# Score products of a Perceiver kernel: all products of a PSUM bank ahead of its reductions, low part last

## The chip, the cores and the metric

The kernel runs on one core of a Trainium2 chip. The metric is the time of one execution on the device in microseconds (us). Before the change three runs gave 2074.91, 2084.85 and 2086.65 us, a median of 2084.85.

## The reference

The input `x` has 8 batches of 64 tokens with 512 features; the context has 8 batches of 1601 rows with 512 features. Three layers follow one another, each with a residual. The change lies in the first, in its cross attention:

```python
kvx = jnp.einsum('bsi,oi->bso', cond, w_kv_x)        # cond is the context
kx, vx = jnp.split(kvx, 2, axis=-1)
kx = _ln(kx.reshape(b, sc, g, d), kxln_w, kxln_b)    # g = 8 groups, d = 128
vx = vx.reshape(b, sc, g, d)
xout = _gqa(qx, kx, vx).reshape(b, s, nh * d)        # nh = 16 heads, two per group
...
def _gqa(q, k, v):
    scores = jnp.einsum('bsghd,btgd->bghst', q, k) / np.sqrt(q.shape[-1])
    p = jax.nn.softmax(scores, axis=-1)
    return jnp.einsum('bghst,btgd->bsghd', p, v)
```

The same layer also has a self attention and a projection with values rounded to fp8; the second layer is a sparse attention with a learned pair score; the third is a feed-forward network with ternary weights.

## The kernel before

**Work items.** The cross attention is cut into 16 objects of class `Cross`, one for each batch and each half of the eight groups (`HG` = 4 groups in a half). In each group the 128 query rows are two heads of 64 tokens. The 1601 context rows are 13 tiles of 128 rows (`TT`, the last of 65), gathered into six chunks (`CHUNKS`): five of two tiles, so 256 columns, and a last one of three, 321 columns, padded to 322.

**One tile's way.** `keys` (L515 on) loads a transposed context tile, splits it into a high part `cThi` (ACT) and the rest `cTlo` (POOL), and multiplies it by the key weights, which are split in the same way: 12 matmuls of 512 columns into a bank `kx` (L528). ACT squares, DVE sums (L534), POOL takes the inverse root (`rqk`, L173), and DVE writes the normalized keys `kn` (L537). One step later `keys_t` transposes `kn` with four PE transposes into another bank `kx` (L219), ACT writes the keys' high part `kthi` (L550), DVE the difference `kf` (L552), ACT the low part `ktlo` (L553). When all tiles of a chunk are there, `scores` makes, for each of the four groups, three products: high queries by high keys (L571), high queries by low keys (L572), low queries by high keys (L573). A reduction on DVE (L574) then copies the group's scores from PSUM to the tile `S` and takes each row's maximum into `cmx`.

**What follows.** 17 steps behind (`LAG`), ACT exponentiates `S` (L584), `probs_t` transposes a tile of it into a bank `pt` (L593), which is split into `phi` (ACT, L596) and `plo` (DVE, L597), and `weigh` multiplies these by the context tile's parts `chi` and `clo` into four banks `acc` (L620 to L622).

**Banks.** PSUM has eight banks of 512 float32 columns a partition. Pool `pm` holds three (`mainp`): scores `s`, transposed probabilities `pt`, and, once `lane["wide"]` is off, the key tiles `kx` (`kxp`) take turns in them. Pool `pacc` holds four, the sums `acc` over the context; pool `pb` holds one for the background work. In a chunk of 256 columns two groups share a bank (`per` = 2), which makes 160 shared banks over the whole run; in the last chunk each group has its own, 64 in all.

**Order.** The main loop walks over all tiles of all work items and calls the steps in a software pipeline; the other layers' work is pumped in between from streams. The order on each engine is chosen when the kernel is built, by a scheduler with its own costs (`schedule_with_timeline_sim=True`), which may place ready instructions ahead of others. It also inserts the waits: an instruction that writes a tile waits for those that still read or write it.

Of the kernel before, what the change touches and what calls it, by code (L numbers as in the profile page):

```python
# [17 lines left out]
ALU = mybir.AluOpType  # L18
# [3 lines left out]
P = 128  # L22
# [7 lines left out]
HG = 4  # L30
# [7 lines left out]
NCH = len(CHUNKS)  # L38
# [19 lines left out]
def tile_perceiver(ctx: ExitStack, tc: tile.TileContext, t: dict):  # L58
    nc = tc.nc
    V, A, GP, PE = nc.vector, nc.scalar, nc.gpsimd, nc.tensor  # L60
# [16 lines left out]
    def nm(s):  # L77
        uid[0] += 1
        return f"{s}_{uid[0]}"

    def ctile(shape, dt, tag):
        return const.tile(shape, dt, tag=tag, name=tag)
# [9 lines left out]
    def mainp(tag="m"):  # L92
        return pm.tile([P, 512], F32, tag="m", name=nm(tag))

    def kxp(tag="kx"):


        if lane["late"] is not None:
            return lane["late"]
        return accp(tag) if lane["wide"] else mainp(tag)  # L100
# [41 lines left out]
    class Late:  # L142
# [13 lines left out]
        ps = staticmethod(lambda tag="b": kxp())  # L156
# [68 lines left out]
    zeros = ctile([P, 1], F32, "zeros")  # L225
# [268 lines left out]
    class Cross:  # L494
# [60 lines left out]
        def scores(self, ci):  # L555
            chunk = CHUNKS[ci]
            cw = sum(TT[tt][1] for tt in chunk)
            hi, lo = self.kt.pop(ci)
            N = cw + (cw & 1)
            if N > cw:  # L560
                GP.memset(hi[:, :, cw:N].bitcast(F32), 0.0)
                GP.memset(lo[:, :, cw:N].bitcast(F32), 0.0)
            sc = mp.tile([P, HG, KTW], F32, tag="S", name=nm("S"), bufs=7)
            self.S[ci] = sc
            per = 512 // N
            for g in range(HG):
                if g % per == 0:
                    bank = mainp("s")
                ps = bank[:, g % per * N:(g % per + 1) * N]
                q = slice(g * P, (g + 1) * P)  # L570
                PE.matmul(ps, lhsT=self.qhi[:, q], rhs=hi[:, g, :N], start=True, stop=False)  # L571
                PE.matmul(ps, lhsT=self.qhi[:, q], rhs=lo[:, g, :N], start=False, stop=False)  # L572
                PE.matmul(ps, lhsT=self.qlo[:, q], rhs=hi[:, g, :N], start=False, stop=True)  # L573
                V.tensor_tensor_reduce(sc[:, g, :cw], ps[:, :cw], zeros.to_broadcast([P, cw]), 1.0, -3.0e38,  # L574
                                       ALU.add, ALU.max, self.mx[:, g * NCH + ci:g * NCH + ci + 1])

        def maxima(self):
            self.nmx = sm("cnm", HG)
# [472 lines left out]
    for g in range(NA + LAG + 3):  # L1051
# [11 lines left out]
        if 0 <= e < NA:  # L1063
# [4 lines left out]
            ci = CHUNK_OF[kE]  # L1068
# [15 lines left out]
        if 0 <= g - 2 < NA:  # L1084
            nS, kS = divmod(g - 2, NT)
            ci = CHUNK_OF[kS]
# [130 lines left out]
```

## Time and profile before

| | |
|---|---|
| median of three runs | 2084.85 us (2074.91 to 2086.65) |
| profiled execution | 2083.31 us, its span 2081.6 us |
| granted TensorE clock | 0.988 of full speed |
| PE busy | 1979.7 us, 95% |
| PE weight loads (PEld) | 1633.8 us, 78% |
| DVE, ACT, POOL busy | 67%, 63%, 46% |
| DMA | 257.34 MB, mean 124 GB/s |
| score products, L571, L572, L573 | 112.7, 109.4 and 109.0 us busy, 384 each |
| score reductions, L574, two shared-bank groups and the last chunk's | 157.1 us busy, 384, 429 ns each |

PE is TensorE's matmul row, PEld its weight loads, which overlap matmuls; DVE is VectorE, ACT ScalarE, POOL GpSimd. A matmul is pipelined: its row's duration reaches beyond the start of the next one, so a busy PE is not a PE at its peak. A wait is idle time of an engine before an instruction, put down to what released it last.

### The profile page before, as it was taken

The numbers are of one execution on the slowest core, as the hardware profiler recorded it, in microseconds if no ns is written. First come the engines' busy times: TensorE is split into PE (matmuls) and PEld (weight loads), VectorE is DVE, ScalarE is ACT, GpSimd is POOL, SyncE is SP. The second block draws the span as 40 slices with busy tenths as digits, with TensorE's granted clock in tenths as the row PEclk, the third lists the DMA queues.
The fourth block names the chain that finished last, engine by engine and source line by source line (L and its number), as shares of the span: only waits on it lengthen the run. The fifth ranks groups of instructions, "written<-read, shape, count | busy, mean of one in ns | idle before, by whom it ended". The sixth has DMA issues, their size and how long they took to land. (4 is left out here: it accounts for less than half of the span.)

```text
span 2081.6 us, 32709 instructions
## 1 busy us (share of the span) xinstructions
PE 1979.7 (95%) x10923; PEld 1633.8 (78%) x10923; DVE 1390.4 (67%) x3344; ACT 1304.4 (63%) x2787; POOL 952.9 (46%) x1018
## 2 busy tenths in 40 slices
PE   5889999999999899999999999999999999999998
PEld 4778878888778788887888888787878778877776
DVE  7876676576676775767777777675755665576665
ACT  5666757677666666665656656666556665566554
POOL 5454545454454444445444544444454445542232
PEclk9999999999999999999999999999999999999999
DMA  5443343444334444544544454432433223333325
GB/s 180 127 116 112 113 124 110 122 135 127 107 117 130 140 144 123 173 133 156 161 142 148 142 176 145 142 106 69 127 104 109 77 77 97 87 93 101 114 69 170
DMA packets 261817, 257.34 MB, mean 124 GB/s; under 512 B 25408, under 2 KB 186304, under 8 KB 261648
## 3 DMA queue, kind: packets, MB, share of 16 engines
q1 hardware_dynamic: 261648, 255.25, 41.1%
q8 instruction: 86, 1.41, 0.3%
q14 instruction: 83, 0.68, 0.1%
HBM read 231.33 MB, written 23.59 MB: 122 GB/s over the span
## 5 line engine op out<-in xcount | busy, mean ns | idle before, releaser
L523 POOL TENSOR_TENSOR cTlo<-cTr,cThi 128x512 fp32r<-128x512 f32 (+1 forms) x208 | 267.6, 1286 | 497.7 <-ACT cThi L522 352.5
L607 POOL TENSOR_TENSOR clo<-cr,chi 128x512 fp32r<-128x512 f32 (+1 forms) x208 | 277.2, 1333 | 292.8 <-ACT chi L606 273.3
L621 PE MATMUL acc<-plo,chi 128*128 128x512 f32 (+1 forms) x832 | 336.0, 405 | 1.5 <-DVE plo L597 1.5
L622 PE MATMUL acc<-phi,clo 128*128 128x512 f32 (+1 forms) x832 | 327.0, 395 | 0.0
L534 DVE TENSOR_REDUCE kxv<-sq 128x4 f32<-128x512 f32 (+1 forms) x208 | 141.9, 682 | 237.3 <-ACT sq L533 236.7
L620 PE MATMUL acc<-phi,chi 128*128 128x512 f32 (+1 forms) x832 | 254.5, 405 | 5.6 <-ACT phi L596 2.9
L528 PE MATMUL kx<-wkhi,cThi 128*128 128x512 f32 (+1 forms) x832 | 242.9, 413 | 13.0 <-DVE kf L552 4.0
L550 ACT ACTIVATE kthi<-kx,cols 128x512 fp32r<-128x512 f32 (+1 forms) x208 | 159.0, 764 | 145.6 <-PE kx L219 144.7
L606 ACT CAST chi<-cr 128x512 fp32r<-128x512 f32 (+1 forms) x208 | 128.4, 617 | 166.9 <-PE acc L621 117.1
L528 PE MATMUL kx<-wklo,cThi 128*128 128x512 f32 (+1 forms) x832 | 229.4, 398 | 0.0
L173 POOL TENSOR_TENSOR rqk<-kxv,mhalf 128x4 f32<-128x4 f32 (+1 forms) x208 | 219.0, 1053 | 17.2
L528 PE MATMUL kx<-wkhi,cTlo 128*128 128x512 f32 (+1 forms) x832 | 225.7, 393 | 0.0
L522 ACT CAST cThi<-cTr 128x512 fp32r<-128x512 f32 (+1 forms) x208 | 125.2, 602 | 126.8 <-PE kx L528 59.9
L574 DVE CUSTOM_DVE_ANT_0 S<-s,zeros 128x256 f32<-128x256 f32 (+1 forms) x384 | 157.1, 429 | 64.4 <-PE s L573 63.2
L584 ACT ACTIVATE S<-S,cnm 128x256 f32<-128x256 f32 (+1 forms) x384 | 196.4, 518 | 1.8 <-DVE cnm L579 1.8
L528 PEld LDWEIGHTS kx<-wklo,cThi 128*128 128x128 f32 (+1 forms) x832 | 155.8, 187 | 40.9 <-POOL wklo L489 0.5
L528 PEld LDWEIGHTS kx<-wkhi,cThi 128*128 128x128 f32 (+1 forms) x832 | 146.8, 188 | 50.1 <-DVE cmx L574 6.8
L620 PEld LDWEIGHTS acc<-phi,chi 128*128 128x128 f32 (+1 forms) x832 | 151.5, 189 | 42.8 <-ACT phi L596 5.8
L552 DVE SCALAR_TENSOR_TENSOR kf<-kx,cols,kthi 128x512 f32<-128x512 f32 (+1 forms) x208 | 150.8, 725 | 49.9 <-ACT kthi L550 49.0
L528 PEld LDWEIGHTS kx<-wkhi,cTlo 128*128 128x128 f32 (+1 forms) x832 | 153.9, 185 | 38.2
L537 DVE TENSOR_TENSOR kn<-kx,rqk 128x512 f32<-128x512 f32 (+1 forms) x208 | 142.5, 685 | 59.0 <-POOL rqk L173 57.9
L621 PEld LDWEIGHTS acc<-plo,chi 128*128 128x128 f32 (+1 forms) x832 | 157.0, 189 | 29.1 <-DVE plo L597 2.2
(320 smaller groups left out, 4120.2 us busy)
## 6 DMA issues: line engine op xcount, KB each, us to landing
cTr<-in_ctxT SPq DMA_DIRECT2D x192, 256.0 KB
cr<-in_ctx SPq DMA_DIRECT2D x192, 256.0 KB
ld<-in_wproj SPq DMA_DIRECT2D x128, 256.0 KB
wv<-in_wkv SPq DMA_DIRECT2D x64, 256.0 KB
tern<-in_ffn_w SPq DMA_DIRECT2D x64, 256.0 KB
wb<-w1t SPq DMA_DIRECT2D x24, 256.0 KB
wb<-w2t SPq DMA_DIRECT2D x24, 256.0 KB
ld<-lnTd SPq DMA_DIRECT2D x19, 256.0 KB
```

The lines of the kernel that those rows point to most:

```text
L173: GP.tensor_tensor(y[:n], v, mhalf[:n, :k], ALU.pow)
L523: GP.tensor_tensor(clo[:, :, :n], raw[:, :, :n], chi[:, :, :n].bitcast(F32), ALU.subtract)
L528: PE.matmul(ps[:n], lhsT=st[:, ic, :n], rhs=mv[:, ic, :], start=k == 0, stop=k == 11)
L537: V.tensor_tensor(v3(kn[:n], HG), v3(ps[:n], HG), r.unsqueeze(2).to_broadcast([n, HG, D]), ALU.mult)
L550: A.activation(hi[:, :, o], v3(pt, HG)[:, :, :n], AF.Identity, bias=hb["kx"], scale=hw["kx"])
L552: V.scalar_tensor_tensor(kf[:, :, :n], v3(pt, HG)[:, :, :n], hw["kx"], hi[:, :, o].bitcast(F32), ALU.mult, ALU.subtract)
L574: V.tensor_tensor_reduce(sc[:, g, :cw], ps[:, :cw], zeros.to_broadcast([P, cw]), 1.0, -3.0e38, ALU.add, ALU.max, self.mx[:, g * NCH + ci:g ...
L584: A.activation(self.S[ci][:, g, :cw], self.S[ci][:, g, :cw], AF.Exp, bias=self.nmx[:, g:g + 1], accum_out=self.su[:, g * NCH + ci:g * NCH ...
L607: GP.tensor_tensor(clo[:n], raw[:n], chi[:n].bitcast(F32), ALU.subtract)
L620: PE.matmul(self.U[ic], lhsT=chi[:n, s], rhs=phi[:n], start=tt == 0, stop=False)
L621: PE.matmul(self.U[ic], lhsT=chi[:n, s], rhs=plo[:n], start=False, stop=False)
L622: PE.matmul(self.U[ic], lhsT=clo[:n, s], rhs=phi[:n], start=False, stop=last)
```

## The change

Within each bank of scores the loops change places. Before, a group's three products are written in the order high-high, high-low, low-high (queries by keys), its reduction follows, and then comes the next group. After it, the high-high products of all groups of the bank come first, then the low queries by high keys, then the high queries by low keys; the reductions of the bank's groups follow together. Only the bank's very first product has the start flag. In the last chunk, with one group to a bank, only the order of the three products changes. Further down, all lines move by two: the reduction is L576 after it.

```diff
             per = 512 // N
-            for g in range(HG):
-                if g % per == 0:
-                    bank = mainp("s")
-                ps = bank[:, g % per * N:(g % per + 1) * N]
-                q = slice(g * P, (g + 1) * P)
-                PE.matmul(ps, lhsT=self.qhi[:, q], rhs=hi[:, g, :N], start=True, stop=False)
-                PE.matmul(ps, lhsT=self.qhi[:, q], rhs=lo[:, g, :N], start=False, stop=False)
-                PE.matmul(ps, lhsT=self.qlo[:, q], rhs=hi[:, g, :N], start=False, stop=True)
-                V.tensor_tensor_reduce(sc[:, g, :cw], ps[:, :cw], zeros.to_broadcast([P, cw]), 1.0, -3.0e38,
-                                       ALU.add, ALU.max, self.mx[:, g * NCH + ci:g * NCH + ci + 1])
+            for g0 in range(0, HG, per):
+                bank = mainp("s")
+                gs = range(g0, g0 + per)
+
+                for k, (a, x) in enumerate(((self.qhi, hi), (self.qlo, hi), (self.qhi, lo))):
+                    for i, g in enumerate(gs):
+                        PE.matmul(bank[:, i * N:(i + 1) * N], lhsT=a[:, g * P:(g + 1) * P], rhs=x[:, g, :N],
+                                  start=k == 0 and i == 0, stop=k == 2, skip_group_check=True)
+                for i, g in enumerate(gs):
+                    ps = bank[:, i * N:(i + 1) * N]
+                    V.tensor_tensor_reduce(sc[:, g, :cw], ps[:, :cw], zeros.to_broadcast([P, cw]), 1.0, -3.0e38,
+                                           ALU.add, ALU.max, self.mx[:, g * NCH + ci:g * NCH + ci + 1])
```

## The prediction

> **What bounds the kernel now.** I read the page's busy shares first, then the list of what TensorE (PE) waited for, then one stretch of the timeline.
>
> ```profile
> PE 1979.7 (95%) x10923; PEld 1633.8 (78%) x10923; DVE 1390.4 (67%) x3344; ACT 1304.4 (63%) x2787; POOL 952.9 (46%) x1018
> ```
>
> PE is busy 95% of the span, no other engine over 67%: PE's instructions, and the roughly 102 us in which it stands, set the time. The change removes no instruction, so all that it can move is those 102 us. The waits of PE, longest first (waiting line, releaser, us in total, times, longest):
>
> ```profile
> PE pt L593 <- DVE cmx L574: 14.0, 16, 1.9
> PE tr L219 <- DVE fa L201: 11.4, 2, 10.4
> PE kx L219 <- DVE kn L537: 10.4, 13, 3.6
> PE kx L219 <- DVE cmx L574: 6.3, 13, 1.5
> PE s L571 <- DVE cmx L574: 6.1, 10, 1.2
> ...
> PE kx L528 <- DVE cmx L574: 4.0, 9, 1.6
> ```
>
> Four of these name one releaser, the score reduction on L574: 14.0 + 6.3 + 6.1 + 4.0 = 30.4 us in 48 waits, the largest single cause. The row of L571 is the score product itself; the others are transposes and key products that write no scores. They wait because they get a PSUM bank that scores held: `s`, `kx` and `pt` share the three banks of pool `pm`. How long scores hold one is seen in one chunk:
>
> ```profile
> 407.20 0.28 PE L571 MATMUL s<-kthi,qxhi 128*128 128x256 f32 x1
> ...
> 408.94 0.28 PE L571 MATMUL s<-kthi,qxhi 128*128 128x256 f32 x1
> ...
> 409.29 0.28 PE L572 MATMUL s<-ktlo,qxhi 128*128 128x256 f32 x1
> ...
> 409.40 0.28 PE L573 MATMUL s<-kthi,qxlo 128*128 128x256 f32 x1
> ...
> 409.72 0.43 DVE L574 CUSTOM_DVE_ANT_0 S<-s,zeros 128x256 f32<-128x256 f32 x1 [0.94 <-PE s L573]
> ...
> 410.07 0.42 DVE L574 CUSTOM_DVE_ANT_0 S<-s,zeros 128x256 f32<-128x256 f32 x1
> ...
> 410.69 0.28 PE L571 MATMUL s<-kthi,qxhi 128*128 128x256 f32 x1
> ...
> 411.24 0.43 DVE L574 CUSTOM_DVE_ANT_0 S<-s,zeros 128x256 f32<-128x256 f32 x1
> ...
> 411.61 0.42 DVE L574 CUSTOM_DVE_ANT_0 S<-s,zeros 128x256 f32<-128x256 f32 x1
> ```
>
> By the order of the built program, 407.20, 409.29 and 409.40 are group 0 in bank A, 408.94 opens group 2 in bank B. The reductions at 409.72 and 410.07 read A and B; only then, at 410.69, group 1 starts in A, three products, and A is read again at 411.24. So a bank goes through products, reduction, products, reduction: 4.5 us here. Matching all score matmuls of the timeline with the program's order, the 160 paired banks live 5.17 us on average, 827 us in sum; in every one the fourth product starts after the first reduction's end, 1.35 us after on average.
>
> **The change part by part.**
>
> *Counts.* 1152 score matmuls and 384 reductions stay, with their shapes and weight loads. Consecutive 256-column products start 0.115 us apart whether they share `qhi` or not (409.29, 409.40, 409.52, 409.64). Cost nothing. ACT, POOL and the DMA queues keep their instructions.
>
> *The turn inside a bank goes.* All six products come before either reduction. The order of the two built programs shows it: in the paired banks 312 score products wait on a DVE semaphore before, 153 after. PE work of other kinds standing between the first and last product of a paired bank (0.23 us per 512-column matmul, 0.12 per 256, 0.11 per transpose, as spaced in the timeline) falls from 460 us over the 160 banks to 105. Of the 6.1 us on L571 I count 5 as gone; the rest belongs to a chunk's first product, which still waits for a free bank.
>
> *The bank's next owner waits less.* For each handover in the pool (the old tile taken as the third before in order of first use), I summed the PE work standing between the last product in the old tile and the first instruction in the new. From scores to `kx` or `pt` there are 197 handovers: median 1.12 (`kx`) and 0.88 us (`pt`) before, 155 of them under 1.5 us. After it is 2.97 and 3.00 us. What has to fit there grows: before, the last reduction ended 1.03 us on average after the last product; after, two reductions follow, 0.35 us more (the spacing 409.72 to 410.07), with a second bank ahead in DVE's queue 1.05. So I count as tight those under 2.0 us: 43. The 14.0 + 6.3 + 4.0 = 24.3 us shrink to 24.3 x 43/155 = 6.7, gain 17.6.
>
> *Refilling the pipe.* A 512-column matmul lasts 0.39 us but the next starts 0.23 after it, so an ended wait saves up to 0.16 us that the idle column does not count. Some 36 of 48 waits go: 36 x 0.16 = 5.8, taken at 5.
>
> *Keys' low part.* Both high-part products no longer stand behind `ktlo`, and PE now goes on to `ktlo` sooner. Today PE waited for `ktlo` (L553) 0.2 us, once. The first low-part product stands 7.60 us of PE work (median) behind the chunk's last key transpose before, 7.61 after, and the chain `kthi`, `kf`, `ktlo` takes 3.4 us on average from start to end. Cost nothing, covered by `kx` and `acc` products between; without that cover each of 96 chunks would cost up to 1.4 us (`kf` and `ktlo`).
>
> *DVE's queue.* Reductions stand closer. Runs of three or four in a row on DVE go from 6 to 52; in 35 of these `kn` (L537) is next, for which the key transposes wait. Two more reductions are 0.7 us. PE waited for `kn` 13 times in 208, so 46 x 13/208 x 0.7 = 2 us lost.
>
> *Given back.* PE, standing less, comes earlier to its other waits (about 70 us of the 102). With no other engine over 67% I take a small part, 4 us; bounds 0 and everything.
>
> Sum: 5 + 17.6 + 5 - 2 - 4 = about 22 us. The profiled run took 2083.3 (span 2081.6 and 1.7 around it): 2061. It lies 1.5 us under the median of the runs, which span 12 us, so I leave it there. Bounds: everything behind L574 with refilling is 30.4 + 48 x 0.16 = 38 us, and a few us more since weight loads waited for L574 in 70 cases, 50.2 us; a gain of 42 gives 2041.
>
> The Trainium skill (Perfetto Trace Analysis, section Matmuls) speaks against this edit: independent matmul groups should rotate through different PSUM banks, so that evacuating one overlaps the next group's products. By it, the edit gives up an overlap of 0.35 us (the trace's spacing) in each of 160 banks, up to 56 us. The rows show no such overlap inside a bank to lose (410.07 to 410.69 above), only that between banks A and B, which stays.
>
> **The rivals.**
>
> *Slower: the burst of reductions holds DVE.* Four reductions in a row keep `kn`, `kf` and `plo` behind them, and PE meets them late: 52 bursts x 0.7 = 36 us lost if PE stands for each. Of the forecast's 27 us gained, this case keeps about the 17.6 of the handovers: +18, 2101. It decides once PE stands the full 0.7 us after more than 25 of the 52 bursts, where the loss passes 17.6. For: the 10.4 us on `kn`, longest 3.6. Against: 13 of 208, and the median `kn` was ready over 6 us before its transposes in the timeline.
>
> *No change: PE's idle time moves.* The waits leave L574 and reappear behind `kn`, `phi` or the casts of ACT, as each context tile's chain (ACT, POOL, DVE) has its own length: 2083 less 0 to 8. For: POOL stood 352.5 us for ACT's cast of `cThi`, a chain with long links. Against: the shares of busy time.
>
> *The scheduler undoes it.* The order on each engine is remade at build. The order shows that it did not: 153 waits, 105 us. But it moved thousands of other instructions, worth a few us either way, in my range.
>
> **How the numbers follow.** A difference of 0.5% (10.4 us) is about what measuring this kernel can tell from none. Forecast, 2041 to 2074: 0.73. No change, 2075 to 2088: 0.16. DVE bursts: 0.08, and a low-part wait or an unlucky order, 0.03, both slower. Hence faster 0.73, same 0.16, slower 0.11. The range 2041 to 2081 holds the forecast's case and half of no change, which leaves out 2 in 10.
>
> **What would show it.** After: L574's successor (L576) behind PE's waits under 15 us instead of 30.4; no wait of a bank's second group; PE's idle time near 80 us; the score products of a bank in an unbroken six or in four plus two; `kn` rows near 10 to 13 us; `ktlo` waits under 2. Wrong if the `kn` row grows past 25, if `ktlo` shows up with over 10, or if PE's idle total stays at 100 under other names.

## The result, and the profile after

The changed kernel takes 2082.43 us (median of 20 runs) against 2085.36 us (20 runs): a ratio of 0.999, 95% interval 0.9979 to 1.0001. That is 3 us where 22 were forecast, and the interval includes 1. The profiled execution took 2080.4 us, its span 2078.6 against 2081.6. One execution of a kernel further down (e3_before_pace) took 2436.56 us at a granted clock of 0.752 and is left out of that kernel's numbers.

The page after: the busy shares are nearly the same.

```profile
span 2078.6 us, 32685 instructions
PE 1972.7 (95%) x10923; PEld 1633.0 (79%) x10923; DVE 1397.7 (67%) x3344; ACT 1302.0 (63%) x2787; POOL 962.0 (46%) x1018
```

PE's waits after (waiting line, releaser, us, times, longest). L576 is the reduction, L595 the transposes into `pt`, L622 the first context product:

```profile
PE tr L219 <- DVE fa L201: 10.7, 2, 10.1
PE pt L595 <- DVE cmx L576: 8.6, 13, 1.5
PE kx L219 <- DVE kn L537: 7.5, 7, 2.7
PE kx L528 <- DVE kf L552: 7.2, 9, 1.6
PE kx L528 <- DVE m1y L431: 6.2, 4, 2.3
...
PE acc L622 <- ACT phi L598: 4.3, 6, 1.5
PE tr L360 <- ACT fa L355: 4.2, 3, 2.6
PE kx L219 <- DVE hag L344: 4.0, 1, 4.0
...
PE kx L219 <- DVE cmx L576: 3.5, 4, 1.5
...
PE kx L528 <- DVE cmx L576: 3.0, 3, 1.3
...
PE s L572 <- DVE cmx L576: 1.2, 1, 1.2
```

The four rows of the reduction fall from 30.4 us in 48 waits to 8.6 + 3.5 + 3.0 + 1.2 = 16.3 in 21. But `kf` rises from 4.0 to 7.2, `phi` from 2.9 to 4.3, `m1y` on key products from 1.5 to 6.2, `fa` of L355 from 1.8 to 5.3 over its lines, and `hag` is new. Two of these rows as they were before (L620 is the later L622):

```profile
PE kx L528 <- DVE kf L552: 4.0, 6, 1.5
...
PE acc L620 <- ACT phi L596: 2.9, 4, 1.2
```

By the page, span less PE's busy time is 105.9 us where it was 101.9: the idle time has other names.

The timeline of PE and DVE after, in one bank of a chunk, shows that the change does what it says:

```profile
507.64 0.40 PE L572 MATMUL s<-kthi,qxhi 128*128 128x256 f32 x2
...
507.88 0.40 PE L572 MATMUL s<-kthi,qxlo 128*128 128x256 f32 x2
...
508.12 0.40 PE L572 MATMUL s<-ktlo,qxhi 128*128 128x256 f32 x2
...
508.80 0.39 DVE L576 CUSTOM_DVE_ANT_0 S<-s,zeros 128x256 f32<-128x256 f32 x1
...
509.12 0.42 DVE L576 CUSTOM_DVE_ANT_0 S<-s,zeros 128x256 f32<-128x256 f32 x1
```

Six products in a row, then both reductions: the bank is held 1.9 us. In the order of the built program 66 of the 160 shared banks have their six products unbroken like this. Over the 160 shared banks, matched with the order of the built program, the mean hold falls from 5.17 to 3.21 us, while the time from the end of a bank's last product to its last reduction's end rises from 1.03 to 1.56.

**How far ahead is PE?** The line of the last context product says when PE is through with the attention (instructions, durations in ns, first and last start in us). Before, then after:

```profile
L622 PE MATMUL acc<-phi,clo x832: 387/393/499, 131.7 to 1955.5; 128*128 128x512 f32 x154, 65*128 65x512 f32 x13
```

```profile
L624 PE MATMUL acc<-phi,clo x832: 387/393/504, 135.8 to 1945.5; 128*128 128x512 f32 x154, 65*128 65x512 f32 x13
```

So PE leads by 10.0 us there, and the rest takes 133.1 us where it took 126.1, with the same 641 PE instructions left. Of the lead of 10.0 us, 3.0 are left at the end of the program.

**An account of the 10 us.** For each PE matmul of the timeline I took the time to the next one's start, less the lower quartile of that spacing for its kind in the kernel before, and sorted what is over by cause, up to that last product; a matmul that starts at half clock goes to the last row, whatever it waited for. It counts refilling too, so its numbers are larger than the idle column's.

| us lost by PE up to the end of the attention | before | after | forecast of the change | measured |
|---|---|---|---|---|
| waits for score reductions | 38.5 | 19.8 | -27.6 | -18.7 |
| all other waits | 55.4 | 70.4 | +6 | +15.0 |
| spacing without a recorded wait | 78.5 | 73.8 | 0 | -4.7 |
| stretches at half clock | 14.7 | 13.5 | 0 | -1.2 |

They sum to -9.6; 0.4 stay unaccounted. So of the forecast's 21.6 us, 8.9 are missing at the reductions and 9.0 at the other waits, 5.9 came unforeseen from the last two rows, and 7.0 went behind the attention.

### The profile page after: what moved, and what is told of

It reads as the page before. It is cut to its first block, busy times and chain, and to the rows that moved or that the text cites. A ratio compares the mean times of both kernels' runs of the same rounds, so it can differ in the third digit from the quotient of the medians.

```text
span 2078.6 us, 32685 instructions
## 1 busy us (share of the span) xinstructions
PE 1972.7 (95%) x10923; PEld 1633.0 (79%) x10923; DVE 1397.7 (67%) x3344; ACT 1302.0 (63%) x2787; POOL 962.0 (46%) x1018
## 4 chain that ended last, share of the span: by engine, by line
PE 45%; DVE 4%; DMA 3%; ACT 1%; issue 1%; POOL 1%; SPq 0%; POOLq 0%; DVEq 0%; ACTq 0%
PE kx L528 13%; PE acc L622 5%; PE acc L623 5%; PE acc L624 4%; PE s L572 3%; PE pt L595 2%; PE pp L417 2%; PE kx L219 2%; PE xo L643 2%; DMA tern<-in_ffn_w 1%; PE p L737 1%; PE p L742 1%; PE y L970 1%; PE y L926 1%; PE fh L988 1%
## 5 line engine op out<-in xcount | busy, mean ns | idle before, releaser
L622 PE MATMUL acc<-phi,chi 128*128 128x512 f32 (+1 forms) x832 | 252.1, 404 | 6.2 <-ACT phi L598 4.3
L173 POOL TENSOR_TENSOR rqk<-kxv,mhalf 128x4 f32<-128x4 f32 (+1 forms) x208 | 221.7, 1066 | 17.1
L622 PEld LDWEIGHTS acc<-phi,chi 128*128 128x128 f32 (+1 forms) x832 | 151.3, 189 | 44.9 <-ACT phi L598 7.0
L624 PEld LDWEIGHTS acc<-phi,clo 128*128 128x128 f32 (+1 forms) x832 | 156.8, 189 | 26.9
```

Source lines behind the costliest of these rows:

```text
L173: GP.tensor_tensor(y[:n], v, mhalf[:n, :k], ALU.pow)
L622: PE.matmul(self.U[ic], lhsT=chi[:n, s], rhs=phi[:n], start=tt == 0, stop=False)
L624: PE.matmul(self.U[ic], lhsT=clo[:n, s], rhs=phi[:n], start=False, stop=last)
```

## The experiments

One table first. "Waits" are PE's idle us for the score reductions (times); "attention" is the start of the last context product, both from the profiled execution. "Clock loss" is (1 - granted clock) x time, the mean over the kernel's runs; it says how much time the throttle could have cost, not how much lay on the path. Ratios are against the kernel before, run on the same chip. The two e11 kernels leave out work.

| kernel | median us | ratio, interval | waits | attention | clock loss |
|---|---|---|---|---|---|
| before | 2085.4 (first 20 runs), 2087.6 (beside the experiments) | | 30.4 (48) | 1955.5 | 24.5 (96 runs beside the experiments) |
| changed | 2082.4 | 0.999, 0.9979-1.0001 | 16.3 (21) | 1945.5 | 32.5 (20 runs) |
| e1_group_only | 2086.7 | 0.999, 0.9972-1.0007 | 17.1 (22) | 1959.3 | 27.1 |
| e2_low_last_only | 2091.6 | 1.0007, 0.9989-1.0025 | 27.1 (42) | 1961.9 | 28.1 |
| e3_before_pace | 2092.5 | 1.0015, 0.9995-1.0035 | 34.6 (50) | 1959.4 | 28.4 |
| e4_after_pace | 2081.6 | 0.9949, 0.9927-0.9971 | 9.8 (20) | 1947.6 | 32.2 |
| e7_before_pace2 | 2095.9 | 1.0047, 1.0032-1.0062 | 29.3 (50) | 1965.9 | 32.0 |
| e8_after_pace2 | 2083.4 | 0.9991, 0.9975-1.0008 | 13.5 (22) | 1950.2 | 32.5 |
| e12_group_only_pace2 | 2085.7 | 0.9991, 0.9975-1.0007 | 16.3 (25) | 1950.7 | 31.9 |
| e13_low_last_pace2 | 2098.6 | 1.0049, 1.003-1.0067 | 28.5 (51) | 1967.8 | 29.6 |
| e5_own_banks | 2093.5 | 1.0039, 1.0023-1.0056 | 33.0 (42) | 1964.7 | 30.6 |
| e6_double_reduction | 2170.8 | 1.0402, 1.0372-1.0432 | 33.3 (42) | 2043.6 | 49.4 |
| e10_sbuf_repeat | 2134.2 | 1.0228, 1.0208-1.0248 | 17.7 (21) | 2005.0 | 47.5 |
| e9_before_pool_ws | 2105.7 | 1.0091, 1.007-1.0112 | 43.4 (52) | 1974.5 | 33.2 |
| e9_after_pool_ws | 2090.9 | 1.0016, 1.0001-1.003 | 9.7 (16) | 1945.1 | 45.0 |
| e11_before_short_end | 2053.8 | 0.983, 0.9814-0.9845 | 31.7 (48) | 1961.5 | 28.8 |
| e11_after_short_end | 2049.8 | 0.9808, 0.979-0.9827 | 15.5 (21) | 1954.2 | 33.8 |

### Each half of the change alone

**e1_group_only**: both groups' products first, in the old order of products.

```diff
-                for k, (a, x) in enumerate(((self.qhi, hi), (self.qlo, hi), (self.qhi, lo))):
-                    for i, g in enumerate(gs):
+                for i, g in enumerate(gs):
+                    for k, (a, x) in enumerate(((self.qhi, hi), (self.qhi, lo), (self.qlo, hi))):
```

> One half of the change alone: both groups' products ahead of the bank's reductions, in the old order of products (high-high, high-low, low-high, group by group). Theory A (the turn inside the bank is what cost; the rest of the forecast gain is given back late, in the last 130 us): the waits of PE for the score reductions fall from 30.4 to 13 to 20 us, the last product of the sixteenth work item comes 5 to 11 us before the 1956 us of the kernel before, total 2075 to 2085 us. Theory B (PE's idle time only changes its name all along the way): the reductions' row falls too, but that last product comes within 4 us of 1956. Theory C (the order of the products matters, the low part last): no lead here, within 3 us.

**e2_low_last_only**: on the kernel before, the second and third product of each group change places.

```diff
-                PE.matmul(ps, lhsT=self.qhi[:, q], rhs=lo[:, g, :N], start=False, stop=False)
-                PE.matmul(ps, lhsT=self.qlo[:, q], rhs=hi[:, g, :N], start=False, stop=True)
+                PE.matmul(ps, lhsT=self.qlo[:, q], rhs=hi[:, g, :N], start=False, stop=False)
+                PE.matmul(ps, lhsT=self.qhi[:, q], rhs=lo[:, g, :N], start=False, stop=True)
```

> The other half alone: the low part of the keys comes last within each group, and each group is still reduced before the next one starts in its bank. Theory A: the waits for the score reductions stay near 30 us, the last product of the sixteenth work item within 4 us of 1956 us, total 2080 to 2090. Theory C: the lead of about 10 us shows up here. Theory B: within 4 us.

Grouping alone took the waits down to 17.1 us, as theory A had it, but PE was not ahead at the end of the attention (1959.3; theory A had 1945 to 1951), and the time, 2086.7, lies above theory A's range: by this one build theory B holds. The order alone left the waits near where they were (27.1), and its time cannot be told from that of the kernel before (0.9989 to 1.0025), though its attention ends 6.4 us later, more than any of the theories allowed. One build each could not say whether the missing lead of e1 was the order of products or the build, so both were repeated at another pace, below.

### The same pair in other built orders

**e3_before_pace, e4_after_pace** (1.6) and **e7_before_pace2, e8_after_pace2** (1.62): one constant, the pace at which the background work is pumped in, on the kernel before and on the changed one.

```diff
-PACE = 1.61, 4
+PACE = 1.6, 4
```

> The kernel before with the pace of the background work 1.60 instead of 1.61 steps a tile: a change of the order of instructions that has nothing to do with scores. It measures how far the time moves when the built order alone changes. Theory A: 2080 to 2095, with 25 to 35 us of waits for the score reductions; it is the partner of the next run. Theory B: anything within 10 us of 2085.

> The changed kernel with the pace of the background work 1.60, the partner of the run above. Theory A: the last product of the sixteenth work item 6 to 13 us earlier than in that run, the waits for the score reductions 12 to 20 us instead of 25 to 35; the total differs from it by anything between -15 and +1, depending on what the end of the kernel does. Theory B: that product within 4 us of the partner's, or later.

> The kernel before with the background's pace 1.62: a third built order of it. Theory A: waits for the score reductions 27 to 40 us, 2080 to 2095 us.

> The changed kernel with the pace 1.62, partner of the run above. Theory A: waits for the score reductions 10 to 20 us; other waits of PE up to the last product of the sixteenth work item about 15 us more than in the partner, as in the two pairs before; that product 5 to 13 us earlier than in the partner; the total 1 to 13 us less. Theory B: that product within 4 us of the partner's.

Against its partner the changed kernel is 10.9 us faster at 1.60 and 12.5 us at 1.62 (by medians), where it was 2.9 at 1.61; at the end of the attention it leads by 11.8 and 15.7 us, where it was 10.0. Theory B (no lead) falls. Theory A holds in the main; it missed the waits at 1.60 (9.8 us, under its 12 to 20), the lead at 1.62 (over its 5 to 13) and, by 1 us, the time of e7_before_pace2. What it had of the other waits holds: by the account above the reductions' waits go from 43.0 to 13.2 and from 37.7 to 17.1 us, and all other waits from 54.0 to 67.7 and from 61.2 to 73.6: +13.7 and +12.4, as +15.0 in the first pair. PE's waits of e8_after_pace2 show the names:

```profile
PE kx L528 <- DVE kf L552: 8.5, 9, 1.6
PE acc L622 <- ACT phi L598: 7.5, 11, 1.7
...
PE tr L360 <- ACT fa L355: 4.5, 6, 2.5
PE pt L595 <- DVE cmx L576: 4.4, 10, 0.6
```

The end of the kernel (span less attention) is longer in each pair: 126.1 to 133.1, 130.1 to 132.9, 124.7 to 129.9 us.

And the partners are slower by their medians than the kernel before itself, the second clear of noise, the first not: its order at 1.61 is the quickest of the three paces, by 4.9 and 8.3 us, and it has the smallest clock loss, 24.5 us against 28.4 and 32.0 at the other paces. The changed kernel loses 32.5, 32.2 and 32.5 us at the three. Time without the clock loss (medians) goes from 2063.3 to 2050.0, from 2064.1 to 2047.2, from 2065.1 to 2051.5: -13.3, -16.9, -13.6. So the three pairs agree there, and the first pair's smaller gain goes with 8.0 us more of clock loss; that this time lay on PE's path is not shown. For the first pair, 24.5 and 2063.3 are of the 96 runs beside the experiments, whose median 2087.6 the changed kernel undercuts by 5.2 us; the clock of the 20 runs of the first comparison is not on record. e4_after_pace is faster than the kernel before by its interval; among versions that do all the work it was the only one.

**e12_group_only_pace2, e13_low_last_pace2**: the halves above, with the pace 1.62.

> The grouping alone (both groups' products ahead of the reductions, in the old order of products) with the pace of the background work 1.62, to be held against the kernel before (2095.9) and the changed kernel (2083.4) at that pace, which lost 32.0 and 32.5 us to the clock. Theory A (the turn inside the bank is the whole matter): within 4 us of the changed kernel, 2080 to 2087. Theory C (without the low part last, the six products of a bank stand apart, so grouping alone brings less than half): 2088 to 2096, with the waits for the score reductions at 15 to 22 us all the same.

> The order of products alone (low part of the keys last, each group still reduced before the next one starts in its bank) at the pace 1.62. Theories A and C both expect it within 5 us of the kernel before at that pace, 2091 to 2101, with 25 to 35 us of waits for the score reductions. If it is at 2088 or less, the order has a worth of its own.

Grouping alone, 2085.7, lies 2.4 us from the whole change at this pace, and its attention ends at 1950.7 against 1950.2. The order alone, 2098.6, lies 2.7 us above the kernel before at this pace. PE's waits of e12_group_only_pace2:

```profile
PE pt L595 <- DVE cmx L576: 8.7, 11, 1.8
...
PE kx L528 <- DVE kf L552: 6.2, 8, 2.0
...
PE acc L622 <- ACT phi L598: 4.0, 8, 0.9
PE kx L219 <- DVE cmx L576: 3.8, 6, 1.4
```

At this pace the grouping carries the gain; theory C is not borne out. That e1 at 1.61 had no lead goes with that build: up to there its profiled execution lost 22.9 us at half clock, 8.2 more than the kernel before, and 18.6 more in other waits. The account of the halves is less even than their times. At 1.62 grouping alone takes the waits for reductions from 37.7 to 20.5 us and the other waits from 61.2 to 65.3; the order alone leaves the first at 36.9 and takes the second to 67.9 (at 1.61, from 55.4 to 62.6). So some of the other waits may come with the order of products; each is a single build.

### The price of a bank, and of DVE

**e5_own_banks**: each group has a bank of its own.

```diff
-            per = 512 // N
+            per = 1
```

> The changed kernel with one bank for each group (per = 1): 384 banks of scores in place of 224, each three products and one reduction. It also has no turn inside a bank, but takes twice as many banks from the same three. Theory A (what counts is how soon the bank's next owner gets it): the PE work between a bank's last score product and its next owner is short again in this build (213 handovers under 1.5 us, against 54 after and 184 before), so the waits for the score reductions are 22 to 35 us and the time 2083 to 2095 us. Theory D (the turn inside the bank was what cost; handovers do not matter): waits under 15 us, time 2070 to 2082.

As theory A said: no turn inside a bank, yet 33.0 us of waits and 2093.5 us. The view of PE's waits shows where they sit:

```profile
PE pt L595 <- DVE cmx L576: 16.6, 16, 2.9
...
PE kx L219 <- DVE cmx L576: 8.3, 12, 2.6
```

Theory D falls: without the turn, the waits at handovers to the next owner are as dear as before. The Trainium skill (Perfetto Trace Analysis, section Matmuls) would have independent groups rotate through different banks; here, with three banks shared with two other kinds of tile, that is 0.39% slower than the kernel before (0.23 to 0.56). This is one build, and the pace alone moved the kernel before by up to 0.47%: it is no faster than the kernel before, and 11 us slower than the changed kernel, whose three builds lie within 2 us.

**e6_double_reduction**: each reduction twice. **e10_sbuf_repeat**: the second one reads the copy in SBUF.

```diff
-                    V.tensor_tensor_reduce(sc[:, g, :cw], ps[:, :cw], ...
+                    for _ in range(2):
+                        V.tensor_tensor_reduce(sc[:, g, :cw], ps[:, :cw], ...
```

```diff
                     V.tensor_tensor_reduce(sc[:, g, :cw], ps[:, :cw], ...
+                    V.tensor_tensor_reduce(sc[:, g, :cw], sc[:, g, :cw], ...
```

> The changed kernel with every score reduction issued twice, the second with the same inputs and outputs: a bank is held 0.35 us longer for each group, and DVE has 134 us more work (67% to 74%). It gives the price of a bank's hold. Theory A: waits for the score reductions rise from 16 to 25 to 40 us and the time by 6 to 16 us, to 2089 to 2099. Theory B (idle time only changes its name): the row rises as much, and the time by less than 4 us.

> The changed kernel with a second reduction for each group that reads the copy in SBUF instead of the bank: as much more DVE work as in the doubled reductions, but a bank is not held for it. It parts the bank's hold from the load on DVE. Theory A (the hold is the price): at most 25 us slower than the changed kernel, waits for the score reductions under 25 us. Theory E (every step that DVE comes late costs, because the other tiles' banks, pt and kx, are also read by DVE): 60 to 95 us slower, as with the doubled reductions (2171 us), with the waits for phi, kf, fa and kn together up by over 20 us.

The first costs 88 us over the changed kernel, the second 52, both far more than theory A allowed; theory E had 60 to 95 for the second, which missed too, while its waits for `phi`, `kf`, `fa` and `kn` came as it said (40.0 to 63.0 us by the view). The second is not the same load, as its text assumes: a reduction of 256 columns takes 523 ns out of SBUF and 418 out of PSUM, and DVE's busy time rises by 181.3 us, against 140.1 in the first. In e10 the waits for the reductions are as they were (17.7), and it is other waits that grew: up to the end of the attention from 70.4 to 110.6 us by the account, and the clock loss from 32.5 to 47.5. The view of its PE waits:

```profile
PE kx L528 <- DVE kf L552: 16.2, 11, 2.5
...
PE acc L624 <- ACT phi L600: 8.4, 13, 1.4
PE kx L219 <- DVE cmx L576: 7.8, 6, 2.7
PE pt L597 <- DVE cmx L576: 7.3, 9, 1.8
```

So more work on DVE, at 74% of this span, costs PE time although no bank of scores is held for it. The first kernel, with less work on DVE and longer holds, is 36.7 us slower still; at the end of the attention it is 38.6 us behind the second, of which the account puts 19.1 to the waits for reductions, 10.6 to half clock and 7.3 to other waits.

**e9_before_pool_ws, e9_after_pool_ws**: 120 splits of projection weights go from DVE to POOL, on each kernel.

```diff
-                    V.tensor_tensor(w2[:, k, 1, :], raw, w2[:, k, 0, :].bitcast(F32), ALU.subtract)
+                    GP.tensor_tensor(w2[:, k, 1, :], raw, w2[:, k, 0, :].bitcast(F32), ALU.subtract)
```

> The kernel before with the split of the projection weights (L409, 120 instructions of 0.69 us, 82 us on DVE between 390 and 1830 us) moved from DVE to POOL. Theory E (DVE's lateness has a price): 15 to 50 us faster than before. Theory A without E: within 10 us.

> The changed kernel with the same split moved from DVE to POOL. Theory E: the waits that grew with the change (phi, kf, fa) shrink again, so it gains 5 to 20 us on its partner above, more than the changed kernel gains on the kernel before (3 us). Theory A without E: the same difference to the partner as in the other pairs, 3 to 13 us, and no gain over the changed kernel.

Theory E failed in its first half: with the splits off DVE, whose busy time falls from 1390.4 to 1319.0 us, the kernel before was 18 us slower, not faster, which misses theory A's 10 us as well. On POOL an instruction of this kind takes 1.30 us instead of 0.69 (the median), and the order was remade; which of the two it was, I did not part. In its second half the gain on the partner lies in theory E's range, but not for its reason: PE's waits for `phi`, `kf` and `fa` did not shrink, they are 36.6 us where the changed kernel has 28.7. As a fourth pair it has the largest lead, 29.4 us at the end of the attention (1974.5 to 1945.1), of which 14.8 us arrive by the medians: the end is 14.1 us longer (22 more PE instructions, 2.4 us of work, are left there), and the clock loss over the runs is 11.8 us larger.

### Without the end

**e11_before_short_end, e11_after_short_end**: the last two feed-forward networks are left out of each.

```diff
-    bgB.add(ffn_tokens(NJ - 2, 1), ffn_tokens(NJ - 1, 2))
+    xr = load(mp.tile([P, 512], F32, tag="ut", name=nm("fx"), bufs=4), xrd[NJ - 2])
+    nc.sync.dma_start(out_d[(NJ - 2) * P:(NJ - 1) * P, :], xr)
+    nc.sync.dma_start(out_d[(NJ - 1) * P:NJ * P, :], ac["rows"])
```

> The kernel before without the feed-forward network of the last two token pairs: their rows are written out as they come from the second layer (256 of the 512 rows lack the third layer). The order of PE's instructions is that of the kernel before up to this end. It is the partner of the next run; both theories expect the last product of the sixteenth work item at 1950 to 1961 us.

> The changed kernel, with the same feed-forward networks left out. Theory A (the lead of about 10 us at the last product of the sixteenth work item is real, and the stretch from there to the second layer's last result keeps most of it, while the feed-forward networks of the end lose 3 to 5): 6 to 12 us faster than its partner. Theory F (whatever the end consists of, its chains give the lead back): less than 5 us faster, with the time from that last product to the end 5 us or more longer than the partner's.

4.0 us faster by medians, under what theory A wanted; the end is 2.1 us longer, under what theory F wanted. Neither holds whole. The lead in the profiled executions is 7.3 us here (1961.5 to 1954.2), with the same order of PE's instructions up to the end as in the first pair, where it was 10.0; so one profiled execution fixes it to a few us only, and the clock loss is again 5.0 us larger in the changed kernel. What the networks themselves took from the lead is 1 to 5 us (4.0 less 2.9 by the medians, 7.0 less 2.1 by the ends).

## Why the prediction was wrong

**What bounds the kernel, the counts, the turn inside the bank, refilling: right.** The turn's term was 5 of 6.1 us; the row is now 1.2. Refilling was 5: the account's gain at the reductions, 18.7 us, is 4.6 more than that of the idle column. Handover to another bank's owner matters more than the turn, as forecast (e5).

**The keys' low part: right as to `ktlo`.** No wait of PE for `ktlo` shows among the rows after. That the order of products costs nothing at all is less sure: alone, it came with 7.2 and 6.7 us more of other waits.

**The handover term was mis-sized.** I had 24.3 us fall to 6.7; they fell to 15.1, a gain of 9.2 instead of 17.6. The step that failed is the limit of 2.0 us under which a handover counts as tight, and the scaling by the number of tight ones alone. Besides, a bank's next owner is not always the third tile after it: by the banks in the built programs that is so for 159 of the 197 handovers before, and for 68 after. By the banks as built, with the forecast's prices, all 38 waits before stand at the 158 handovers with under 1.5 us of work; after, 11 of the 20 waits (10.6 us) stand at the 51 under 2.0, and 9 (4.5 us) between 2.2 and 2.8, where I had counted none. The reductions end 1.56 us after the last product instead of 1.03. A part of the miss is the built order: at the other paces the same three rows fell from 25.6 to 9.8 and from 22.0 to 10.6 us.

**"Given back", 4 us, was the other large miss.** With the 2 us for DVE's queue the forecast had 6 us of other waits more; up to the end of the attention they are +15.0, +13.7 and +12.4 us in three pairs. The tiles that PE then waits for do come later: in the timeline ACT starts `phi` 0.59, 0.63, 0.66 us after the transposes' end where it was 0.50, 0.49, 0.49; `plo`, which frees the bank `pt`, ends 2.66, 2.72, 2.70 us after them where it was 2.35, 2.33, 2.38; and `kf`, which frees a key bank, ends 2.47, 2.48, 2.50 us after its transposes where it was 2.26, 2.26, 2.31 (means of 208 each). For `phi` and `kf` the halves with grouping have 0.61 and 0.58, 2.40 and 2.42; those without 0.48 and 0.44, 2.26 and 2.27. So in the builds with grouping the two other kinds of bank come free 0.1 to 0.4 us later a tile. It is not reductions that stand in the way: between the end of `kthi` and the start of `kf` DVE spends 0.05 us on them, where it was 0.08, and 0.57 on other work, where it was 0.43 (first pair). That this is because PE then runs closer to ACT and DVE is argued, not shown, and so is that it makes up all of the other waits: grouping alone at 1.62 has the delay and only 4.1 us of them, the order alone has them without the delay. My reason, no other engine is over 67%, did not hold: in e10 more work on DVE, at 74%, cost 52 us. Shares of busy time do not say how late an engine is.

**The end and the clock were not in the sum.** The end took 7.0, 2.8 and 5.2 us more in three pairs, and the clock loss over all runs rose by 8.0, 3.8 and 0.5 us. The traces tell what the end is longer by. From the last context product on, time at half clock goes from 17.5 to 23.3, from 17.5 to 25.7 and from 13.3 to 20.5 us; half of that rise, an estimate of its cost, is 2.9, 4.1 and 3.6 us. PE's idle time there goes from 9.9 to 15.0, from 12.8 to 12.6 and from 9.4 to 14.2 us. Why the clock is halved for longer there stays open.

**The rivals.** "PE's idle time moves" (0.16) is the case that came, under the very sign I had named for being wrong: the total stayed at 100 under other names. But it is half of the truth, since in five pairs the changed kernel is faster each time, by 2.9, 10.9, 12.5, 14.8 and 4.0 us (the first not clear of noise). "DVE bursts" did not come: idle time of PE before a DVE step with two or more reductions in the 3 us before it fell from 5.3 to 3.2 us, and the `kn` row of the key transposes from 10.4 to 7.5. And "an unlucky order, worth a few us either way" was too small: the kernel before at 1.61 had the best of three orders, by 4.9 and 8.3 us, and any edit of it draws again.

## What to carry to other kernels

Where a scheduler remakes the order at build, one build of each kernel is one draw: vary an unrelated constant on both, and compare pairs. A wait taken away from the engine that bounds the kernel did not pay in full here: other waits took back 12 to 15 us. Look at how late the engines come that free its next buffers (transposes to reader, last product to reduction's end), not at their busy share. Read the granted clock of many runs beside the time: a gain of 13 us without the clock loss came out as 3 to 5.

## What the runs showed of the hardware

The clock was halved for 3.41 us, or a multiple, after stretches in which PE was partly idle, most of them without a long gap. The changes of the clock in the trace stand on a grid of 3.41 us. In the changed kernel from 100 us on, it was halved after eleven stretches of that grid, in each of which PE was busy for 0.16 to 0.54 of the time, the longest gap 2.3 us in all but the last; of the other stretches at full clock only two were as low (0.44 and 0.54). Other builds have exceptions the other way, in e8_after_pace2 up to 0.98. The changed kernel around 944.6 us (columns: length, then busy us of PE, its weight loads, DVE, ACT and POOL, granted clock, DMA share, GB/s):

```profile
941.20:944.60 3.40, 1.54 (x6) 0.74 (x5) 2.83 (x6) 2.37 (x5) 1.57 (x2) 1.00 0.76 241
944.60:948.00 3.40, 3.40 (x10) 2.65 (x9) 3.40 (x5) 0.52 (x1) 3.05 (x2) 0.50 0.60 172
```

And PE's timeline there:

```profile
943.96 0.50 PE L622 MATMUL acc<-phi,chi 128*128 128x512 f32 x1 [1.15 <-ACT chi L608]
...
944.53 0.54 PE L622 MATMUL acc<-phi,chi 128*128 128x512 f32 x1
944.87 0.63 PE L623 MATMUL acc<-plo,chi 128*128 128x512 f32 x1
945.30 0.63 PE L622 MATMUL acc<-phi,chi 128*128 128x512 f32 x1
```

PE was busy 1.54 of 3.40 us, its longest gap 1.15 us; then products of 512 columns start 0.43 us apart instead of 0.23. By an estimate, half of its length, every such stretch costs some 1.7 us on top of the stalls before it, and the sum depends on which stalls fall together; the clock loss of the builds that do all the work goes from 24.5 to 49.4 us. The Trainium skill (TensorE: Matmul & The Clock Gate, section HAM oscillation) puts the rule as no PE-idle gaps over about 3.4 us; here a stretch half idle in shorter gaps was enough.
